# Sixth pair's projections, first output rows, and the three parts of a held group: three moves in the order of a layer-norm, state-space and mixture-of-experts kernel

## The chip, the cores and the metric

One core of a Trainium2 chip runs the whole program. The metric is the device time of one execution in microseconds (us). A span is the time from the first to the last instruction of one profiled execution; the device time of that execution is a little longer.

## The reference, cut to what matters

For 16 sequences of 512 tokens with 256 numbers each:

```python
xn = layernorm(x)
# state space: Bu = xn @ B_w.T (64 states), h[t] = sigmoid(log_lambda) * h[t-1] + Bu[t]
y  = h @ C_w.T + D * xn
# mixture of experts, 8 experts, top 1, with a capacity for each expert and sequence
aff      = (xn @ waff.T) / (|xn| * |waff| + 1e-9)
tcr      = one_hot(argmax(softmax(aff)))
cap      = clip(floor(512 * sigmoid(mean(aff) - threshold)), 4, 512)
dispatch = tcr * (rank of aff along the sequence < cap)
ffn = sum over e of ( gelu((xn * dispatch[e]) @ W1[e] + b1[e]) @ W2[e] + b2[e] )
out = x + y + ffn
```

An expert maps 256 to 1024 to 256. A token that an expert does not take still gets that expert's answer to a zero row, so the kernel gives every token the sum of all experts' answers to zero (`call`) and, for a token that was taken, adds its own expert's answer less that expert's answer to zero (`zb`).

## The kernel before, in words

**Front.** The 16 sequences are eight pairs of sequences, numbered q = 0 to 7 (HQ = 4, so HQ + 2 is pair 6 and HQ + 3 is pair 7). For each pair, `load_x` fetches the rows and `load_xt` the transposed rows, 1 MB each, over SP's DMA queue. `project` (L243) multiplies the transposed rows by `proj`: part 0 gives the affinity numerators in a bank of `ps_m`, part 1 the 64 state inputs in a bank of `ps_f`, both banks single; ScalarE (ACT) copies each out (`npart`, `bur`), and ACT's queue writes `npart` to `numr`. `scaled` brings the norms to the other layout, `recur` (L359) multiplies and scans on VectorE (DVE), and `outputs` (L367) multiplies a pair's states by C_w in two parts (`py`, 8 matmuls each), copies them on ACT and writes the rows to `row_d`. `py0` shares its bank with the norms of pair 1 until `recur(1)` has read them.

**Routing and steps.** `first_routing` gives the first half of the tokens to 9 groups of two tiles of 128 tokens ("pairs", steps 0 to 8). `second_routing` packs the rest into 23 pairs (steps 9 to 31) and single tiles (steps 32 to 36). A step does, for its group: `turned` transposes the normalised rows (`px` on TensorE (PE), copied to `xsT` on DVE) one step ahead; `hidden` (L882) runs four stages 0 to 3 of W1 (`ph`, then Gelu on ACT into `hs`), and then one stage for each tile (4, and 5 for a pair) of W2 (`po`). After each stage a function `between(stage, event)` issues what is to lie there: weights for step i + 2 (`fetched`, four parts, SP queue), row gathers for step i + 3 (`gathered`, GpSimd (POOL), one indirect DMA for a tile), the transposes for step i + 1, and in steps 0 to 3 what the front has left over (`left_out`, L1329: outputs and recurrences of the pairs). Steps 0 to 8 keep their answers (`held_y`); the rows of `row_d` and the capacities are not ready yet.

**Dealt work.** From step 1 on three generators, `capacity` (L1002), `second_routing` (L637) and `capacity_mask` (L1048), are dealt out by `fill` (L1213) after each stage. A ledger `lead` sets how much: `pe(...)` adds what PE work has been issued, `dve(...)` takes off what DVE work has been issued, and `fill` draws from the first generator that is not waiting while `lead` is above 0. A generator that yields a number has issued that much DVE work; one that yields `None` is passed over for the rest of this call. What of `lead` is not drawn is dropped. Before step 9 `drained` (L1228) issues all that is left, with no stage between.

**Held groups.** From step 10 on the held groups j = 0 to 8 are finished beside the later steps, in three turns: turn 0 gathers their two tiles of x rows, turn 1 their two tiles of `row_d` rows (both on POOL, behind the last stage's event), turn 2 loads the expert's `zb1`, and at the step's end does the DVE work `normal`, `rests`, `finish` and the two scatters to the output. `held_turns` (L1411) says which turns lie beside which step: even groups have turns 0 and 1 beside one step and turn 2 beside the next, odd groups one beside each of three, all of it beside the pairs, steps 10 to 31.

Within the two blocks the order on PE, DVE, POOL and SP is the order of the text, each engine and each queue taking its own in order. A PSUM bank of a pool with one buffer is given on when the last reader of its tile is done: `pn`, `pp`, `pv2`, `ps_s` and `pk` use that of `ps_m`; `pa`, `pm` and the accumulator `pz` of the bias shares (from step 4 on) use that of `ps_f`.

Of the kernel before, what the change touches and what calls it, by code (L numbers as in the profile page):

```python
# [15 lines left out]
P = 128  # L16
B, S, D = 16, 512, 256
NS = 64
# [41 lines left out]
def ssm_moe_kernel(  # L60
# [166 lines left out]


    NQ = B // 2
    known, nparts = {}, {}  # L230
    xts, x4s, burs, hTs, halfs, prss, rows_out = {}, {}, {}, {}, {}, {}, {}

    def load_x(q, x4=None):
        for h in range(2):
            t = x4[h] if x4 else fx.tile([P, NC, D], F32, name="x4", bufs=4)
            nc.sync.dma_start(out=t, in_=xp[q].rearrange("p (h c d) -> p h c d", h=2, c=NC)[:, h])
            x4s[q, h] = t

    def load_xt(q, xt2=None):
        xts[q] = xt2 or fx.tile([P, 2, ND, S], F32, name="xt2", bufs=2)  # L240
        nc.sync.dma_start(out=xts[q], in_=xt[q].rearrange("p (h dc s) -> p h dc s", h=2, dc=ND))

    def project(q, parts=(0, 1)):  # L243

        for part in parts:
            pb = (ps_m, ps_f)[part].tile([P, S], F32, name="pb", tag="mf"[part])
            pe(1.9)
            m = (32, NS)[part]
            cols = slice(0, NS) if part else slice(NS, NS + m)
            for dc in range(ND):  # L250
                for h in range(2):
                    nc.tensor.matmul(
                        out=pb[h * m : (h + 1) * m, :],
                        lhsT=proj[:, dc, cols],
                        rhs=xts[q][:, h, dc, :],
                        start=(dc == 0),
                        stop=(dc == ND - 1),
                    )
            if part:
                burs[q] = held.tile([P, S], F32, name="bur", tag="y")  # L260
                nc.scalar.copy(burs[q], pb)
                continue
            npart = nparts[q] = fin.tile([2 * m, S], F32, name="npart", bufs=2)
            nc.scalar.copy(npart, pb[: 2 * m, :])
            if q >= NQ // 2:
                for h in range(2):
                    k = 2 * q + h
                    nc.scalar.dma_start(out=numr[k * NE : (k + 1) * NE, :], in_=npart[h * m : h * m + NE, :])
# [149 lines left out]
    def ranks(hf, rt, banks, tags):  # L418
# [33 lines left out]
        if hf:  # L452
            pn = banks[0].tile([P, NC, HB * NE], F32, name="pn", tag=tags[0])
            rows = slice(hf * HB * NE, (hf + 1) * HB * NE)
            numc = numr.rearrange("k (c p) -> k c p", c=NC)
            for c in range(NC):
                nc.tensor.transpose(pn[:, c, :], numc[rows, c, :], ident[rows, rows])
            yield None
        aff3 = aff[:, hf].rearrange("p c b e -> p (c b) e")
        if hf:  # L460
            nc.vector.tensor_tensor(aff3, den, pn.rearrange("p c (b e) -> p (c b) e", e=NE), ALU.mult)
# [369 lines left out]
        return load_w2, products, folded, shares  # L831


    def behind(transfer, event):

        if event is not None:
            tc.add_manual_dep(
                transfer.ins,
                event.ins.name,
                mybir.DependencyInfo(mybir.DependencyClass.Sync, mybir.DependencyReason.DATA),  # L840
                reason="begun where the queues have room",
            )

    def gather(t, src, idx, event=None):
        begun = nc.gpsimd.indirect_dma_start(  # L845
            out=t, out_offset=None, in_=src, in_offset=bass.IndirectOffsetOnAxis(ap=idx, axis=0)
# [155 lines left out]
    def capacity(mk):  # L1002

        while "affinities" not in known:
            yield None
        affc = mk.tile([P, NC, P], F32, name="affc", tag="affc")
        nc.vector.tensor_copy(
            affc.rearrange("p c (h k) -> p h c k", h=2), aff.rearrange("p h c b e -> p h c (b e)")
        )
        yield 0.8  # L1010
        cap = small(mk, "cap", 1)
        col = small(mk, "col", 1)
        nc.vector.tensor_reduce(col, aff.rearrange("p h c b e -> p (h c b e)"), AX.X, ALU.add)
        yield 0.8
        yield None
        pa = ps_f.tile([P, S], F32, name="pa", tag="f")
        for c in range(NC):
            nc.tensor.transpose(pa[:, c * P : (c + 1) * P], affc[:, c, :], ident)
        row = known["row"] = mk.tile([P, S], F32, name="row")
        nc.vector.tensor_copy(row, pa)  # L1020
        yield 0.8
        yield None
        yield None

        pm = ps_f.tile([P, 1], F32, name="pm", tag="f")
        nc.tensor.matmul(out=pm, lhsT=ones, rhs=col, start=True, stop=True)
        yield None
        nc.vector.tensor_scalar(cap, pm, 1.0 / (NT * P * NE), thr_sb, ALU.mult, ALU.subtract)
        nc.scalar.activation(cap, cap, AF.Exp, scale=-1.0)
        yield 0.2  # L1030
        yield None
        yield None
# [12 lines left out]
        known["capacity"] = cap  # L1045
        yield 0.8
# [118 lines left out]
    def span(i):  # L1165

        g = order[i] - NP1
        return (2 * i, 2) if g < 0 else (2 * g, 2) if g < NP2 else (NP2 + g, 1)
# [65 lines left out]
    with front_pools:  # L1234
# [4 lines left out]
        with tc.manual_schedule(engines={PE, DVE, ACT, POOL, SP}):  # L1239
# [6 lines left out]
            def quarter(t, k):  # L1246
                return t[:, k * NC * D : (k + 1) * NC * D].rearrange("p (c d) -> p c d", c=NC)
# [11 lines left out]
            xt_late = [hid.tile([P, 2, ND, S], F32, name="xt_late", tag="hs") for j in range(2)]  # L1259
            load_x(HQ + 2, [quarter(x_late, k) for k in (0, 1)])  # L1260
            load_xt(HQ + 2, xt_late[0])
            load_x(HQ + 3, [quarter(x_late, k) for k in (2, 3)])
            load_xt(HQ + 3, xt_late[1])

            moments(0)
            roots(0)
# [22 lines left out]
            routing = first_routing(rt1)  # L1289
            for meanwhile in (  # L1290
                lambda: None,
                lambda: (project(HQ), recur(0), project(HQ + 1)),
                lambda: None,
            ):
                while next(routing) is not None:
                    pass
                meanwhile()
# [6 lines left out]
                    gathered(0, what, None, (s,))  # L1304
            scaled(2, ps_h, "ph")
            scaled(3, ps_h, "ph")
            project(HQ + 2)
            recur(1)
            recur(2)
            xns[0], events[0, "xn"] = normal(*rows[0][:2], 1)  # L1310
            first, events[0, "xsT"] = turned(xns[0], 1, ps_x)
# [1 line left out]
            recur(3)  # L1313
            gathered(1, 0, events[0, "xn"])
            gathered(1, 1, events[0, "xsT"])
            fetched(1, None, events[0, "xsT"])

            def second_tile():
                normal(*rows[0][:2], 2, 1, xns[0])
                turned(xns[0], 2, None, 1, first)  # L1320
                moments(HQ)
                roots(HQ)
                moments(HQ + 1)
                normed(1)
# [2 lines left out]


            left_out = {  # L1329
                (0, 0): [(0, 0)],  # L1330
                (0, 1): [(0, 1)],
                (0, 2): [(1, 0)],
                (0, 3): [(1, 1)],
                (0, 4): [(2, 0)],
                (0, 5): [(2, 1)],
                (1, 0): [(3, 0)],
                (1, 1): [(3, 1)],
                (2, 0): [(4, None)],
# [59 lines left out]
    with (  # L1398
# [8 lines left out]
        NW = 6  # L1407
        held_rows = {}


        held_turns = {}  # L1411
        beside = [i for i in range(NP1 + 1, steps) if span(i)[1] == 2]
        for j in range(NP1):
            for turns in ((0, 1), (2,)) if j % 2 == 0 else ((0,), (1,), (2,)):
                held_turns[beside.pop(0)] = j, turns
        with tc.manual_schedule(engines={PE, DVE, POOL, SP}):
            load_w2, products, folded, shares = bias_shares(fp)
            for k in range(3):
# [1 line left out]
            for i in range(EARLY, steps):  # L1420
# [11 lines left out]
                def between(stage, event):  # L1432
                    if stage < NPART:
                        fetched(i + 2, stage, event)
                    if stage == 1:
                        gathered(i + AHEAD, 0, event)
                        turn(i + 1, (ps_x, ps_x2)[i % 2])
                    if stage == 3:
                        gathered(i + AHEAD, 1, event)
                    for turn_of in turns:  # L1440
                        if turn_of == 2 or stage != (4 if turns == (0, 1) and turn_of == 0 else 5):
                            continue
                        if turn_of == 0:
                            held_rows[j] = rows_of(x_rows, row_d, inv1, 2 * j, 2, [event, event])
                        held_rows[j][2](turn_of)
                    k = stage - 2 + NW * (i - EARLY)
                    if 0 <= k < pieces:
                        products(k)
                        pe(0.6)
                        if k + 3 < pieces:  # L1450
                            load_w2(k + 3)
                    if k == pieces - 1:
                        folded()
                    if k == pieces + 2:
                        shares()
# [82 lines left out]
```

## Time and profile before

| | |
|---|---|
| median of 3 runs | 628.13 us (624.35 to 629.61) |
| the profiled execution's own time | 626.64 us |
| its span | 624.9 us |
| granted TensorE clock, mean | 0.988 |
| PE matmul busy | 591.9 us (95%) |
| DVE, ACT, POOL busy | 368.3, 169.5, 265.2 us |

Times in the views are counted from the span's start. A line of a timeline gives start, length, engine, line, operation, output and input tiles and how many instructions are merged; in brackets stands how long the engine was idle just before and what ended that. In a table by windows the figures are busy time of each engine, the granted clock of TensorE (1.00 is full), the share of the DMA engines' time and the rate in GB/s. Steps begin with PE's first `ph` of a group: step 0 at 60.70, step 3 at 126.42, step 9 at 247.76, step 10 at 263.77, step 11 at 278.02, step 31 at 567.82, and the singles 32 to 36 at 581.85, 589.10, 596.34, 603.59 and 610.83.

### The profile page before, as it was taken

The numbers are of one execution on the slowest core, as the hardware profiler recorded it, in microseconds if no ns is written. First come the engines' busy times: TensorE is split into PE (matmuls) and PEld (weight loads), VectorE is DVE, ScalarE is ACT, GpSimd is POOL, SyncE is SP. The second block draws the span as 40 slices with busy tenths as digits, with TensorE's granted clock in tenths as the row PEclk, the third lists the DMA queues.
The fourth block names the chain that finished last, engine by engine and source line by source line (L and its number), as shares of the span: only waits on it lengthen the run. The fifth ranks groups of instructions, "written<-read, shape, count | busy, mean of one in ns | idle before, by whom it ended". The sixth has DMA issues, their size and how long they took to land. (4 is left out here: it accounts for less than half of the span.)

```text
span 624.9 us, 9629 instructions
## 1 busy us (share of the span) xinstructions
PE 591.9 (95%) x3163; PEld 475.3 (76%) x3163; DVE 368.3 (59%) x975; ACT 169.5 (27%) x406; POOL 265.2 (42%) x274
## 2 busy tenths in 40 slices
PE   5877999989999998999999999999999999999995
PEld 2224768758776677888888888888888888888995
DVE  5976745499878876536347373546447374463541
ACT  2224533344112230222222222222222222222331
POOL 1104782212222121365565555665566655535511
PEclk9897999999999999999999999999999999999999
DMA  8986676857677642475676666766665766767790
GB/s 331 373 324 242 256 279 243 250 200 275 216 280 254 244 158 97 177 238 211 223 251 237 233 246 236 257 235 233 221 237 212 245 222 228 250 215 243 252 319 7
DMA packets 48260, 147.62 MB, mean 236 GB/s; under 512 B 8861, under 2 KB 14864, under 8 KB 46160
## 3 DMA queue, kind: packets, MB, share of 16 engines
q1 hardware_dynamic: 35072, 109.00, 48.5%
q0 software_dynamic: 11504, 29.10, 14.1%
q10 hardware_dynamic: 1632, 8.88, 3.7%
q8 instruction: 26, 0.43, 0.3%
q14 instruction: 26, 0.21, 0.1%
HBM read 129.81 MB, written 17.65 MB: 236 GB/s over the span
## 5 line engine op out<-in xcount | busy, mean ns | idle before, releaser
L898 PE MATMUL ph<-xsT,ws 128*128 128x256 f32 (+1 forms) x1216 | 259.8, 365 | 4.9 <-ACT hs L907 4.4
L918 PE MATMUL po<-ws,hs 128*128 128x256 f32 x1104 | 247.3, 380 | 0.0
L898 PEld LDWEIGHTS ph<-xsT,ws 128*128 128x128 f32 x1216 | 212.1, 191 | 39.4 <-ACT hs L907 7.4
L918 PEld LDWEIGHTS po<-ws,hs 128*128 128x128 f32 x1104 | 208.0, 190 | 32.0 <-issue 3.6
L907 ACT ACTIVATE hs<-ph,ws 128x256 f32<-128x256 f32 (+1 forms) x304 | 121.1, 451 | 327.5 <-issue 203.3
L845 POOL DMA_INDIRECT sums<-in_xp_dram,inv_g x51 | 53.9, 1058 | 77.3 <-ACT hs L907 62.9
L984 DVE TENSOR_TENSOR w<-po,zb 128x512 f32<-128x512 f32 (+1 forms) x28 | 18.0, 644 | 110.2 <-PE po L918 77.1
L845 POOL DMA_INDIRECT yr<-row_d,inv_g x51 | 51.2, 1005 | 53.5 <-ACT hs L907 40.4
L991 POOL DMA_INDIRECT out_dram<-sums,inv_s x51 | 51.1, 1002 | 51.4 <-DVE sums L987 38.3
L880 DVE COPY xsT<-px 128x512 f32<-128x512 f32 (+1 forms) x38 | 24.4, 641 | 78.5 <-PE px L876 44.9
L845 POOL DMA_INDIRECT xs<-in_xp_dram,inv x18 | 19.5, 1082 | 74.2 <-ACT hs L907 31.2
L987 DVE SCALAR_TENSOR_TENSOR sums<-w,mslot,sums 128x256 f32<-128x256 f32 x69 | 30.6, 482 | 1.3
L958 DVE TENSOR_SCALAR xn<-sums,yr 128x256 f32<-128x256 f32 x69 | 25.9, 414 | 6.8 <-DMA yr<-row_d,inv_g 6.8
L845 POOL DMA_INDIRECT st<-st_d,inv x18 | 18.0, 999 | 24.7 <-DVE cap_i L1037 9.5
L991 POOL DMA_INDIRECT out_dram<-sums,out x18 | 18.2, 1013 | 22.8 <-DVE sums L987 20.0
L845 POOL DMA_INDIRECT sums<-in_xp_dram,inv x18 | 17.0, 946 | 19.3 <-PE po L918 15.0
L975 DVE TENSOR_TENSOR sums<-sums,call 128x512 f32<-128x512 f32 (+1 forms) x37 | 24.3, 657 | 1.3
L974 DVE TENSOR_TENSOR sums<-sums,v 128x512 f32<-128x512 f32 (+1 forms) x37 | 24.3, 656 | 1.3
L972 DVE TENSOR_TENSOR sums<-sums,yr 128x512 f32<-128x512 f32 (+1 forms) x37 | 24.3, 656 | 1.2
L973 DVE TENSOR_TENSOR v<-xn,d_sb 128x512 f32<-128x512 f32 (+1 forms) x37 | 24.3, 655 | 0.0
L876 PE MATMUL px<-ident,xn 128*128 128x128 f32 x138 | 21.7, 274 | 2.5 <-DVE xn L958 2.4
L1079 DVE TENSOR_SCALAR_CACHE_REDUCE junk<-srow,cand 128x512 f32<-128x512 f32 x31 | 23.1, 746 | 1.1
(282 smaller groups left out, 409.7 us busy)
## 6 DMA issues: line engine op xcount, KB each, us to landing
ws<-in_w_dram SPq DMA_DIRECT2D x148, 513.0 KB
row_d<-yrow ACTq DMA_DIRECT2D x8, 1040.0 KB
x<-in_xp_dram SPq DMA_DIRECT2D x12, 512.0 KB
w2s<-in_w_dram SPq DMA_DIRECT2D x16, 384.0 KB
zb<-z_d SPq DMA_DIRECT2D x37, 128.0 KB
early<-in_xt_dram SPq DMA_DIRECT2D x4, 1024.0 KB
xt<-in_xt_dram SPq DMA_DIRECT2D x2, 1024.0 KB
x_late<-in_xp_dram SPq DMA_DIRECT2D x4, 512.0 KB
```

The costliest lines, as they stand in the source:

```text
L845: begun = nc.gpsimd.indirect_dma_start(out=t, out_offset=None, in_=src, in_offset=bass.IndirectOffsetOnAxis(ap=idx, axis=0))
L880: return into, nc.vector.tensor_copy(xsT[:, :, cols], px[:, :, cols])
L898: nc.tensor.matmul(out=ph[:, k, cols], lhsT=w1s[:, dc * NF + c * P : dc * NF + (c + 1) * P], rhs=xsT[:, dc, cols], start=(dc == 0), stop=( ...
L907: event = nc.scalar.activation(hs[:, c, cols], ph[:, k, cols], AF.Gelu, bias=b1s[:, c : c + 1])
L918: event = nc.tensor.matmul(out=po[:, s, :], lhsT=hs[:, c, s * P : (s + 1) * P], rhs=w2s[:, c * D : (c + 1) * D], start=(c == 0), stop=(c = ...
L958: event = nc.vector.tensor_scalar(xn[:, s, :], xs[:, s, :], st[:, s, 0:1], st[:, s, 2:3], ALU.subtract, ALU.mult)
L972: nc.vector.tensor_add(r, r, yr[:, :n, NST:])
L973: nc.vector.tensor_tensor(v[:, :n, :], xn[:, :n, :], over(d_sb), ALU.mult)
L974: nc.vector.tensor_add(r, r, v[:, :n, :])
L975: nc.vector.tensor_tensor(r, r, over(call), ALU.add)
L987: nc.vector.scalar_tensor_tensor(out=r[:, s, :], in0=v[:, s, :], scalar=mslot[:, k0 + s : k0 + s + 1], in1=r[:, s, :], op0=ALU.mult, op1=A ...
L991: put = nc.gpsimd.indirect_dma_start(out=out, out_offset=bass.IndirectOffsetOnAxis(ap=inv[:, k0 + s : k0 + s + 1], axis=0), in_=r[:, s, :] ...
```

## The change

- The projection matmuls of pair 6 (`project(HQ + 2)`) are issued straight behind those of pair 5, while the first routing is under way; their copies out of PSUM (`projected`) stay where they were. `outputs(0)` moves from stages 0 and 1 of step 0 to between `recur(1)` and `recur(2)`, ahead of step 0, and the other entries of `left_out` for step 0 move up by two stages.
- Pair 7's loads (2 MB) leave the first run of loads; they are issued in `second_tile`, behind the normalisation of step 0's second tile, and step 1's weights follow them on the same queue (before, these were issued behind the copy of the first tile).
- In the dealt work, `second_routing` waits three calls of `fill` rather than one between the transposes `pn` and the DVE work that reads them, and `capacity` four calls rather than none between `pa` and its reader.
- Each held group's three turns lie beside three steps in a row, from step 10 to step 36, single tiles among them.

```diff
-    def project(q, parts=(0, 1)):
+    def project(q, parts=(0, 1), copied=True):
         for part in parts:
-            pb = (ps_m, ps_f)[part].tile([P, S], F32, name="pb", tag="mf"[part])
+            pb = pbs[part] = (ps_m, ps_f)[part].tile([P, S], F32, name="pb", tag="mf"[part])
...
+            if copied:
+                projected(q, (part,))
+
+    def projected(q, parts=(0, 1)):
+        for part in parts:
+            pb = pbs[part]
...
                 nc.tensor.transpose(pn[:, c, :], numc[rows, c, :], ident[rows, rows])
-            yield None
+            for _ in range(3):
+                yield None
...
             nc.tensor.transpose(pa[:, c * P : (c + 1) * P], affc[:, c, :], ident)
+        for _ in range(4):
+            yield None
         row = known["row"] = mk.tile([P, S], F32, name="row")
...
             load_x(HQ + 2, [quarter(x_late, k) for k in (0, 1)])
             load_xt(HQ + 2, xt_late[0])
-            load_x(HQ + 3, [quarter(x_late, k) for k in (2, 3)])
-            load_xt(HQ + 3, xt_late[1])
...
-                lambda: (project(HQ), recur(0), project(HQ + 1)),
+                lambda: (project(HQ), recur(0), project(HQ + 1), project(HQ + 2, copied=False)),
...
             scaled(3, ps_h, "ph")
-            project(HQ + 2)
+            projected(HQ + 2)
             recur(1)
+            outputs(0)
             recur(2)
...
-            fetched(1, None, events[0, "xsT"])
             def second_tile():
-                normal(*rows[0][:2], 2, 1, xns[0])
+                _, event = normal(*rows[0][:2], 2, 1, xns[0])
+                load_x(HQ + 3, [quarter(x_late, k) for k in (2, 3)], event)
+                load_xt(HQ + 3, xt_late[1])
+                fetched(1, None, event)
...
             left_out = {
-                (0, 0): [(0, 0)],
-                (0, 1): [(0, 1)],
-                (0, 2): [(1, 0)],
-                (0, 3): [(1, 1)],
-                (0, 4): [(2, 0)],
-                (0, 5): [(2, 1)],
+                (0, 0): [(1, 0)],
+                (0, 1): [(1, 1)],
+                (0, 2): [(2, 0)],
+                (0, 3): [(2, 1)],
...
-        held_turns = {}
-        beside = [i for i in range(NP1 + 1, steps) if span(i)[1] == 2]
-        for j in range(NP1):
-            for turns in ((0, 1), (2,)) if j % 2 == 0 else ((0,), (1,), (2,)):
-                held_turns[beside.pop(0)] = j, turns
+        held_turns = {NP1 + 1 + k: (k // 3, (k % 3,)) for k in range(3 * NP1)}
...
-                        if turn_of == 2 or stage != (4 if turns == (0, 1) and turn_of == 0 else 5):
+                        if turn_of == 2 or stage != 3 + n:
                             continue
```

More of the change, by code (lines that the diff above doesn't have):

```diff
@@ L229, in ssm_moe_kernel, with behind, load_x @@
     NQ = B // 2
-    known, nparts = {}, {}
+    known, nparts, pbs = {}, {}, {}
     xts, x4s, burs, hTs, halfs, prss, rows_out = {}, {}, {}, {}, {}, {}, {}
-    def load_x(q, x4=None):
+    def behind(transfer, event):
+        if event is not None:
+            tc.add_manual_dep(
+                transfer.ins,
+                event.ins.name,
+                mybir.DependencyInfo(mybir.DependencyClass.Sync, mybir.DependencyReason.DATA),
+                reason="begun where the queues have room",
+            )
+    def load_x(q, x4=None, event=None):
         for h in range(2):
             t = x4[h] if x4 else fx.tile([P, NC, D], F32, name="x4", bufs=4)
-            nc.sync.dma_start(out=t, in_=xp[q].rearrange("p (h c d) -> p h c d", h=2, c=NC)[:, h])
+            behind(nc.sync.dma_start(out=t, in_=xp[q].rearrange("p (h c d) -> p h c d", h=2, c=NC)[:, h]), event)
             x4s[q, h] = t
@@ L258, in project @@
                     )
+            if copied:
[3 more added lines that the diff above has]
+            pb = pbs[part]
+            m = (32, NS)[part]
             if part:
@@ L831, in bias_shares @@
         return load_w2, products, folded, shares
[L834 to L842, printed above, removed]
     def gather(t, src, idx, event=None):
@@ L1408, in ssm_moe_kernel @@
         held_rows = {}
-        held_turns = {}
-        beside = [i for i in range(NP1 + 1, steps) if span(i)[1] == 2]
-        for j in range(NP1):
-            for turns in ((0, 1), (2,)) if j % 2 == 0 else ((0,), (1,), (2,)):
-                held_turns[beside.pop(0)] = j, turns
+        held_turns = {NP1 + 1 + k: (k // 3, (k % 3,)) for k in range(3 * NP1)}
+        assert NP1 + 3 * NP1 < steps
         with tc.manual_schedule(engines={PE, DVE, POOL, SP}):
```

## The prediction, made before the result was known

> **What bounds the kernel now.** I read the page's first part, then who waited for whom on PE, then PE's timeline for each wait, then the other engines there. The chain that ended last is no help here: it holds only the last scatter.
>
> ```profile
> span 624.9 us, 9629 instructions
> PE 591.9 (95%) x3163; PEld 475.3 (76%) x3163; DVE 368.3 (59%) x975; ACT 169.5 (27%) x406; POOL 265.2 (42%) x274
> ```
>
> PE is busy 95%, so a microsecond counts only if it leaves PE's order of work or closes one of PE's few waits.
>
> ```profile
> PE pv L625 <- DVE lo L545: 5.2, 3, 4.3
> PE ph L898 <- ACT hs L907: 4.4, 5, 1.0
> PE px L876 <- DVE xn L958: 2.4, 1, 2.4
> PE pk L1134 <- DVE mp L1142: 1.5, 5, 0.8
> ```
>
> Each line is a total, a number of waits and the longest. The change touches all four places. The first, in the front:
>
> ```profile
> 49.40 0.36 PE L625 MATMUL pv<-pt,lo 128*128 128x36 bf16 x8 [4.26 <-DVE lo L545]
> ...
> 51.92 3.68 PE L331 MATMUL prs<-ident,mvr 128*64 128x128 f32 x32
> 55.53 4.28 PE L252 MATMUL pb<-xt_late,proj 128*32 128x512 f32 x16
> 59.75 0.44 PE L876 MATMUL px<-ident,xn 128*128 128x128 f32 x2
> ```
>
> PE idles from 45.14 to 49.40; the projections of pair 6 (`xt_late`) come later, right before `px`. The same 32 `prs` matmuls took 2.07 at 20.63, so 3.68 is a slow clock:
>
> ```profile
> 46.00:48.00 2.00, 0.00 (x0) 0.00 (x0) 1.97 (x4) 1.95 (x7) 0.00 (x0) 1.00 0.98 303
> 50.00:52.00 2.00, 1.28 (x26) 1.02 (x28) 1.07 (x2) 1.54 (x4) 0.00 (x0) 0.50 0.78 293
> 54.00:56.00 2.00, 2.00 (x18) 1.39 (x16) 1.97 (x3) 0.00 (x0) 1.64 (x2) 0.50 1.01 408
> ```
>
> Third figure from the end: the granted clock, 1.00 in the hole and 0.50 from 50 to about 57. The other places, from PE's and DVE's timelines:
>
> ```profile
> 58.83 0.41 DVE L958 TENSOR_SCALAR xn<-xs,st 128x256 f32<-128x256 f32 x1 [2.72 <-DMA st<-st_d,inv]
> ...
> 122.01 0.69 DVE L1020 COPY row<-pa 128x512 f32<-128x512 f32 x1 [8.31 <-PE pa L1018]
> ```
> ```profile
> 132.49 0.87 PE L876 MATMUL px<-ident,xn 128*128 128x128 f32 x4 [2.35 <-DVE xn L958]
> ```
> ```profile
> 243.81 0.89 PE L1134 MATMUL pk<-mp,lo 128*128 128x53 bf16 x16 [0.77 <-DVE mp L1142]
> ...
> 284.75 1.99 PE L898 MATMUL ph<-xsT,ws 128*128 128x256 f32 x8 [0.83 <-ACT hs L907]
> ```
> ```profile
> 595.28 0.41 DVE L958 TENSOR_SCALAR xn<-sums,yr 128x256 f32<-128x256 f32 x1 [3.55 <-DMA yr<-row_d,inv_g]
> ```
>
> In order: the first tile's `xn` waits for a gather; DVE stands 8.3 us in its own order for `pa`, and `xn` of step 4 behind it makes PE wait 2.35; the drain before step 9 goes at DVE's pace; a hole of 0.83 to 0.84 stands in steps 11, 16, 21 and 26, each right after a step with turns 0 and 1 together; and among the singles gathered rows come late.
>
> **The change part by part.** The sum is made against the profiled execution, 626.64 us (span 624.9); that is 1.5 below the median of 628.13, within the runs' 624.35 to 629.61.
>
> *A. Front.* Pair 6's 16 projection matmuls take 3.75 (half of 7.49 for 32 at 37.65), so from 45.14 they end at 48.9, inside the hole; they wait for ACT's copies of pair 5, done at 43.9 and 45.9, and for `xt_late`, whose load was issued at 32.85, before the DMA share sank to 0.20 at 42 to 44. `pv` is set by DVE's `lo` and stays. PE's path from 51.92 is then `prs` (2.07 to 3.68), half of `outputs(0)` 1.13, two ACT copies 1.07, the other half 1.13: 5.4 to 7.0, so PE is free for `px` at 57.4 to 59.0. `xn` needs the gather of `st`, issued by 55.05, landed at 58.8 while the DMA share was 1.01; pair 7's 2 MB, now not ahead of step 0's weights, free that stretch. Landing lies between 55.05 and 58.8, so `px` starts between 57.4 (the PE path) and 59.3 against 59.75: a gain of 0.45 to 2.3. I take 1.5, between the ends, since the clock can go either way. ACT's Gelu table load (1.28) follows the last `py` copy as it now follows `bur`: no cost. `outputs(0)`'s 2 x 1.13 leave step 0: 2.27 more. Of the rest, pair 7's three loads and step 1's four weight loads queue on SP from about 61: 4.2 MB at the 300 to 400 GB/s shown is 11 to 14 us, landing by 75; first needed are the moments of pair 7 (78.3 now, the rows come first) and step 1 (88.46 now), so nothing. POOL's gathers for step 1 keep their order and start earlier. Together -3.8 (-2.7 to -4.6).
>
> *B. Later reading of `pn` and `pa`.* DVE no longer stands for `pa`. Walking the ledger call by call (it reproduces where `pn`, `pp`, `pa`, `pm`, `ps_s` and `pk` now stand), `pa` falls to step 2 stage 5 and its reader to step 3 stage 4. Behind `pp` DVE then has `recur(6)` 1.9, 2.3 of `run` to `left` and `xn` 0.73, some 5 us, where PE has 9 before `px` of step 4. So -2.35 (0 to -2.35: next late would be `xn` again).
>
> *C. `pm` meets `pz`.* By the ledger `pm` falls to step 4 stage 1, its reader on DVE to stage 2; there the products of the bias shares first use the same bank and must wait for that reader. DVE has `xsT` 0.69, 1.7 of `eq` and `pt`, and `cap` 0.21 behind `px`; PE 0.27 and 1.95. Cost 0.45 (0 to 1.5, if DVE lags). Behind the waiting products PE's whole order is held.
>
> *D. Drain.* The three calls for `pn` drop some 6 us of the ledger (nothing else can be dealt there), so the mask comes later: by the ledger `ps_s` falls to step 8 stage 5, and `own`, `mtok` and the four `mp` of the first table join the drain. Now the second table's `mp` start 0.48 after step 8's last `po` (242.69) and step 9's `ph` at 247.76. Then: `ps_s` 0.64 to `own`, 0.72 and 0.72 for `own` and `mtok`, then the four `mp` of 0.27, each pair waiting for a `pk` of 0.35, and `mslot` 0.18, about 2.0: the second table's start moves 3.6 later. PE's 0.44 for `ps_s` and 0.95 of `pk` leave step 8. Net +2.2 (1.3 to 3.9: step 9's first 16 `ph` take 5.37 at half clock there, 3.62 later, so 1.75 of slow clock may come on top or half of it go).
>
> *E. Holes.* Four of 0.84 follow steps with eight gathers in one go on POOL (four of the step, four held); the 12 steps of odd groups, six gathers or fewer, show none. The change has six at most, so all go: -3.35 (0 to -3.35; not below, as nothing else stands there).
>
> *F. Held groups among the singles.* Turn 2 is DVE's 0.73 + 2.75 + 1.57 = 5.05. A single step has 7.25 of PE and 3.4 of DVE. Group 7's `row_d` rows are gathered at 589.7 to 592.0, behind step 35's; those were issued 588.0 to 589.0 and read at 595.28, 6.3 later, so group 7's come at 598.3 and its DVE work ends at 603.4. `finish` of step 33 and `xsT` of step 35 queue behind it: 0.9 + 0.42 gives 604.75 where PE wants it at 603.59: 1.2 (0 to 2.5). On POOL four scatters, group 8's x rows and a scatter then push its `row_d` gathers to 611.0 to 613.5. DMA is idle by then (share 0.10); landed at 615.2, 5.05 of DVE, then the last step's 0.9, to 621.15; three scatters, last at 622.5 against 619.42. So +3.1 at the end with the 1.2 in it (2.0 to 4.0). The earlier pair steps carry no more than odd groups now do: nothing.
>
> Sum: -3.8 - 2.35 + 0.45 + 2.2 - 3.35 + 3.1 = -3.75, so 622.9.
>
> A rule at the clock: the rows show 0.50 from 50 to 57 after a hole of 4.26, and 0.50 from 248 to 251 behind the drain. [...]
>
> **The rivals.**
>
> *Holes stay (chance 0.2).* They could come from the state of PE's signals, not from the gathers: ACT and DVE, waiting for PE, both go on at 283.9, though PE's row ends its first stages earlier. Against it: exactly the four steps behind double turns. 622.9 + 3.35 = 626.2.
>
> *Slower: late rows among the singles (0.12).* DMA share is 0.93 to 1.00 from 590 to 608, and groups 7 and 8 add eight gathers of 0.13 MB. Each microsecond that group 7's rows land after 597 passes through DVE's order to `xsT` of step 35 and so to PE. From a landing 10.1 after issue (6.3 + 3.8) the kernel is slower than before; at double the latency, 12.6, it is 622.9 + 6.3 = 629.2. Against it: the extra bytes are some 12% of the 2.2 MB that a single step moves.
>
> *The clock stays halved (0.12).* [...] A at -2.7, D at +3.9: 622.9 + 1.1 + 1.7 = 625.7.
>
> *The front and the tail at their good ends (0.15).* Gather at once, `xsT` of step 35 in time: A -4.6, F +2.0, D +1.3: 622.9 - 0.8 - 1.1 - 0.9 = 620.1.
>
> **How the numbers follow.** My forecast has 0.41: 622.9, by itself 621 to 625. Leaving out about 0.1 at each side, 619.5 to 629.0 takes in the good end and all but the far part of the late rows. About 1% (6.3) of the median is what a measurement can tell from no change: faster means below 621.85, slower above 634.4. Below 621.85 lie most of the good end and a third of the forecast, 0.28; above 634.4 only an extreme of the late rows, 0.03; 0.69 between.
>
> **What would show it.** A: no hole of 4 us before `pv`, clock 1.00 at 50 to 53, step 0 starting at 58.5 to 60, step 1 some 4 us earlier. B: no wait at `px` in step 4. C: a wait of about 0.5 at the first `pz`. D: `ps_s` behind step 8's last `po`, some 8 us of sparse `pk`. E: no holes of 0.84 every fifth step. F: a wait for `xsT` at step 35, three scatters after the last `po`. I am wrong if the holes come back elsewhere, if the bank of `pm` costs PE more than 2 us, or if step 35 waits more than 4.

## The result, and the profile after

The changed kernel takes 623.96 us (median of 20 runs, 617.9 to 630.02) beside 626.48 for the kernel before on the same chips (20 runs). The ratio is 0.9939, with a 95% interval of 0.9918 to 0.996: about 0.6% faster, inside the 1% called no change. The ratio is taken over fast executions alone, which leaves out four of the changed kernel (627.2 to 630.02). The profiled execution has a span of 620.9, 4.1 below that of before, where the sum had forecast 3.75 less. That the sum came out so close is in part luck: by the table below A and E came out 1.8 and 1.4 better than forecast, and F 3.0 worse.

PE's step starts (first `ph` of a group) cut both spans into the same stretches:

| stretch | before | after | difference | forecast |
|---|---|---|---|---|
| start to step 1 | 88.46 | 82.83 | -5.63 | A -3.8 |
| step 1 to step 8 | 136.62 | 134.40 | -2.22 | B, C -1.9 |
| steps 8 and 9, with the drain | 38.69 | 41.10 | +2.41 | D +2.2 |
| step 10 to step 31 | 304.05 | 299.31 | -4.74 | E -3.35 |
| step 31 to the last `po` | 50.34 | 56.46 | +6.12 | F +3.1, tail included |
| last `po` to the end | 6.77 | 6.77 | 0.00 | in F |

The first part of the page shows that most of this is PE's waiting; its work is the same 3163 matmuls, and it is busy only 0.8 less:

```profile
span 620.9 us, 9634 instructions
PE 591.1 (95%) x3163; PEld 475.9 (77%) x3163; DVE 369.7 (60%) x975; ACT 169.9 (27%) x406; POOL 262.8 (42%) x274
```

A. PE's timeline of the changed front. The hole of 4.26 ahead of `pv` has become 0.56, and `py` (the first output rows) stands ahead of `px`:

```profile
48.01 0.37 PE L644 MATMUL pv<-pt,lo 128*128 128x36 bf16 x8 [0.56 <-DVE lo L564]
...
50.49 3.00 PE L349 MATMUL prs<-ident,mvr 128*64 128x128 f32 x32
53.42 1.72 PE L399 MATMUL py<-cw_sb,hT 64*128 64x256 f32 x8
55.82 1.61 PE L399 MATMUL py<-cw_sb,hT 64*128 64x256 f32 x8 [0.67 <-ACT yrow L403]
57.36 0.44 PE L885 MATMUL px<-ident,xn 128*128 128x128 f32 x2
58.32 2.05 PE L907 MATMUL ph<-xsT,ws 128*128 128x128 f32 x16 [0.52 <-issue]
```

The same place by windows; the third figure from the end of a row is the granted clock:

```profile
50.00:52.00 2.00, 1.92 (x34) 1.79 (x32) 1.33 (x4) 0.66 (x2) 0.73 (x1) 0.81 0.11 34
52.00:54.00 2.00, 2.00 (x17) 1.60 (x16) 1.97 (x3) 0.70 (x2) 1.39 (x3) 0.50 0.30 83
54.00:56.00 2.00, 1.33 (x9) 0.82 (x6) 1.09 (x2) 0.82 (x2) 1.69 (x2) 0.84 0.04 1
```

A mean of 0.81 over 2 us is 0.76 us of half clock; with 2.0 and 0.64 from the other rows that is 3.4 us, where before had about 7.

B and C. PE's timeline at step 4's transposes, with no wait in brackets any more, and at the first product of the bias shares, with a new one:

```profile
124.35 0.60 PE L885 MATMUL px<-ident,xn 128*128 128x128 f32 x4
...
146.87 0.61 PE L829 MATMUL pz<-w2s,gb 128*8 128x256 f32 x6 [0.67 <-ACT hs L916]
```

The row names ACT's `hs`, but that one runs until 147.08; the reader of `pm` on DVE, whose bank `pz` takes over, ends at 146.77, 0.10 ahead of `pz`.

D. The drain on PE: `ps_s` and the first table's `pk` have joined it, behind the last `po` of step 8:

```profile
230.78 2.75 PE L927 MATMUL po<-ws,hs 128*128 128x256 f32 x12
233.37 0.60 PE L1125 MATMUL ps_s<-ident,sel 128*128 128x128 f32 x4
235.81 0.56 PE L1145 MATMUL pk<-mp,lo 128*128 128x18 bf16 x16 [1.84 <-DVE mp L1153]
236.57 0.56 PE L1145 MATMUL pk<-mp,lo 128*128 128x18 bf16 x16 [0.20 <-DVE mp L1153]
237.90 0.89 PE L1145 MATMUL pk<-mp,lo 128*128 128x53 bf16 x16 [0.77 <-DVE mp L1153]
...
242.25 5.45 PE L907 MATMUL ph<-xsT,ws 128*128 128x256 f32 x16
```

E and F. From step 10 to step 31 PE waits nowhere. Among the singles it waits four times:

```profile
579.68 1.13 PE L927 MATMUL po<-ws,hs 128*128 128x256 f32 x4 [1.46 <-ACT hs L916]
...
587.04 1.99 PE L927 MATMUL po<-ws,hs 128*128 128x256 f32 x8 [0.48 <-issue]
...
600.92 1.16 PE L907 MATMUL ph<-xsT,ws 128*128 128x128 f32 x8 [1.71 <-issue]
...
604.94 1.99 PE L927 MATMUL po<-ws,hs 128*128 128x256 f32 x8 [1.13 <-ACT hs L916]
```

Steps 32, 33 and 35, in which they stand, take 8.98, 8.23 and 10.65 in place of 7.25, which makes the 6.1. None of the four is the forecast wait for `xsT`. ACT's timeline says what ACT waited for:

```profile
579.26 0.63 ACT L916 ACTIVATE hs<-ph,ws 128x128 f32<-128x128 f32 x2 [2.97 <-PE po L927]
...
600.24 0.63 ACT L916 ACTIVATE hs<-ph,ws 128x128 f32<-128x128 f32 x2 [2.24 <-PE ph L907]
```

In step 32 PE's last two `ph` that ACT waits for had ended at 575.40 and 575.62; the Gelu starts at 579.26, 3.6 later, though ACT has nothing else to do. The trace also records when PE's signal (the semaphore that ACT, DVE and POOL wait on) was raised. Six raises stand due, and none is made until all six are, together:

```
signalling matmuls of PE end: 575.40 575.62 576.92 577.35 577.78 578.22
PE's signal is raised:        579.19 579.24 579.31 579.36 579.40 579.44
```

POOL's row shows a run of five indirect transfers, with no more than 0.3 between them, from 572.11 that ends at 578.23, 0.96 before the first raise. The trace does not hold every raise (331 for 382 signalling matmuls), so a signal is called late below only where an engine that waits for it starts late too.

### The profile page after: what moved, and what is told of

It is laid out like the page before. It is cut to its first block, busy times and chain, and to the rows that moved or that the text cites. A ratio compares the mean times of both kernels' runs of the same rounds, so it can differ in the third digit from the quotient of the medians.

```text
span 620.9 us, 9634 instructions
## 1 busy us (share of the span) xinstructions
PE 591.1 (95%) x3163; PEld 475.9 (77%) x3163; DVE 369.7 (60%) x975; ACT 169.9 (27%) x406; POOL 262.8 (42%) x274
## 5 line engine op out<-in xcount | busy, mean ns | idle before, releaser
L854 POOL DMA_INDIRECT sums<-in_xp_dram,inv_g x51 | 51.7, 1014 | 72.0 <-ACT hs L916 50.5
L403 ACT COPY yrow<-py 128x512 f32<-128x512 f32 x32 | 17.2, 591 | 17.8 <-PE py L399 14.5
```

The lines of the kernel that those rows point to most:

```text
L854: begun = nc.gpsimd.indirect_dma_start(out=t, out_offset=None, in_=src, in_offset=bass.IndirectOffsetOnAxis(ap=idx, axis=0))
```

## The experiments

**The parts.** The first four kernels put the change together from its parts.

e1: the changed kernel with the held turns of before.

```diff
-        held_turns = {NP1 + 1 + k: (k // 3, (k % 3,)) for k in range(3 * NP1)}
-        assert NP1 + 3 * NP1 < steps
+        held_turns = {}
+        beside = [i for i in range(NP1 + 1, steps) if span(i)[1] == 2]
+        for j in range(NP1):
+            for turns in ((0, 1), (2,)) if j % 2 == 0 else ((0,), (1,), (2,)):
+                held_turns[beside.pop(0)] = j, turns
...
-                        if turn_of == 2 or stage != 3 + n:
+                        if turn_of == 2 or stage != (4 if turns == (0, 1) and turn_of == 0 else 5):
```

> The changed kernel with the held turns of the kernel before (two parts together beside every even group, all beside pairs): the parts A to D alone. Theory (long runs of POOL's indirect transfers make PE's signals late, and a long run stands behind a double turn and, in the changed kernel, among the singles): steps 10 to 30 get the four holes back, +4.7 against the changed kernel, and the singles take 50.3 again in place of 56.5, -6.1: about 1.4 below the changed kernel, 622.5, singles 50.3. Rival (the singles' 6.1 come from what the front and drain shifted, not from the held work): the singles stay near 56 and the time is 4.7 above the changed kernel, 628.7.

e2: the kernel before with the held turns of the changed one (the same edit, the other way).

> The kernel before with only the held turns of the changed kernel: parts E and F alone. Theory: -4.7 in steps 10 to 30, +6.1 among the singles: about 1.4 above the kernel before, 627.9. Rival (the gain in steps 10 to 30 or the loss among the singles depends on the rest of the change): between 621.7 (only the gain) and 632.6 (only the loss).

e4: one waiting call for `pn`, four for `pa`.

```diff
-            for _ in range(3):
-                yield None
+            yield None
```

> The changed kernel with one waiting call between the transposes pn and their reader again (before: one, changed: three), the four calls for pa kept. Theory (the three calls drop part of the ledger, which pushes the mask's first table into the drain): the drain before step 9 is 2.3 shorter, the wait at px of step 4 stays away since it was pa's: 2.3 below the changed kernel, 621.7. Rival (the later reading of pn is what removed the wait of 2.35 at px in step 4): the drain's 2.3 are won and 2.35 lost again, no difference.

e5: the kernel before with the front of the changed one.

> The kernel before with part A alone (projections of pair 6, first output rows, pair 7's loads); pn, pa and the held turns as before. Theory (A is worth about 3.9 up to the start of step 1, read from profiles of four kernels with A and two without; the four holes and the wait at px of step 4 stay): 3.9 below the kernel before, 623.5. Rival (part of A's gain is given back in steps 1 to 9, by pair 7's late loads or since the drain takes up what the front leaves): 1 to 2 below, 626; or the wait of 2.35 at px in step 4 goes with A alone, 621.1.

The kernels ran on several chips, each beside the kernel before (medians there 626.61 to 628.91), so the ratios are what compares. The last four columns are from the profiles.

| kernel | median us | ratio to before (95%) | step 1 starts | steps 1 to 9 | 10 to 30 | 31 to last `po` |
|---|---|---|---|---|---|---|
| before | | | 88.46 | 175.31 | 304.05 | 50.34 |
| changed | 623.96 | 0.9939 (0.9918 to 0.996) | 82.83 | 175.50 | 299.31 | 56.46 |
| e1 | 623.19 | 0.9939 (0.9913 to 0.9964) | 85.98 | 175.18 | 304.06 | 50.34 |
| e2 | 627.75 | 1.0015 (0.999 to 1.0039) | 88.72 | 175.88 | 299.30 | 54.00 |
| e4 | 621.42 | 0.9912 (0.988 to 0.9944) | 85.78 | 171.98 | 299.31 | 56.29 |
| e5 | 623.35 | 0.9946 (0.9922 to 0.997) | 84.90 | 175.45 | 304.02 | 50.34 |

The front alone (e5) is worth 626.61 x 0.0054 = 3.4, and the wait at `px` of step 4 stays in it, 2.35. Its ratio lies inside the changed kernel's interval: the other three parts together bring nothing that can be told from noise. The held turns bring the four holes back in e1 and take them away in e2, 4.75 each time; they cost 6.1 among the singles in the changed kernel and 3.7 in e2. So they are no gain: in e1, without them, the kernel is as fast as the changed one within the interval (1.4 less had been expected, which these times could not tell). In e4 the wait at `px` stays away though `pn` is read as early as before, so it was the calls for `pa` that removed it, and those for `pn` are what lengthens steps 1 to 9, by 3.5. The rival expected of e4 (won and lost again) is refuted by the profile; the intervals of the two ratios overlap, so the times alone would not show it.

**What makes the holes.** e3, e6 to e8, e10 and e11 ask what the held parts do to PE.

e3: held work beside pairs only, no step with two gathering turns, turn 2 of an even group beside turn 0 of the next.

```diff
...
+        for j in range(NP1):
+            for turn_of in range(3):
+                held_turns.setdefault(at, []).append((j, turn_of))
+                if turn_of < 2 or j % 2 == 1:
+                    at += 1
...
```

> The changed kernel with all held work beside pairs again, steps 9 to 31, never two gathering turns beside one step: turn 2 of an even group lies beside the same step as turn 0 of the next group, so that in such a step POOL issues six gathers and four scatters rather than eight gathers and two scatters. Theory 1 (what makes PE's signals late is a long unbroken run on POOL, and the scatters of turn 2 come at another time of the step, after DVE's work): no holes among the pairs but perhaps half of them, singles back at 50.3: about 6 below the changed kernel, 618. Theory 2 (the count of indirect transfers in a step decides, ten as before): four holes of 1.2 come back: -6.1 + 4.9, about 622.8. Rival (DVE's held work makes the late signals): as theory 2 or more, since DVE's work then falls together with gathers.

Measured 621.55, ratio 0.9908 (0.9879 to 0.9937). The singles are back at 50.34, and two steps behind each of the four merged ones stands a step of 14.89 to 14.95, 0.67 too long: half a hole, between the two theories, so this one told them apart poorly.

e6: e1, with the held gathers of the double turns as plain transfers on SP's queue.

```diff
...
+                            t, src = ((held_rows[j][0], x_rows), (held_rows[j][1], row_d))[turn_of]
+                            begun = nc.sync.dma_start(out=t[:, s, :], in_=src[(2 * j + s) * P : (2 * j + s + 1) * P, :])
...
```

> The kernel of the first experiment (held turns as before, five double turns), with the eight row transfers of each double turn's two gathering parts issued as plain transfers on SP's queue rather than as indirect ones on POOL: the same bytes at the same event, POOL's run shorter by four. The held tokens of the even groups take other rows than theirs. Theory 1 (POOL's indirect transfers make PE's signals late): all four holes of 1.2 go, steps 11, 16, 21 and 26 at 14.25, 617.7 to 618.5 against 623.2. Theory 2 (the load on the DMA engines does it): the holes stay, 15.4.

e7 and e10: e1, with three or five fills on POOL for each such gather.

```diff
...
+                            for k in range(3):
+                                behind(nc.gpsimd.memset(t[:, s, :], 0.5), event if s == k == 0 else None)
```

> The kernel of the first experiment, with the four indirect transfers of each double turn replaced by twelve fills of the same tiles on POOL (about 0.4 each from the fill of a 128 x 128 tile at 0.20, so 4.7 of unbroken work, as the transfers were 5.0): POOL's run as long as before, four transfers fewer. The held tokens of the even groups are computed from constants. Theory 1a (POOL's run as such makes PE's signals late): holes of about 1.2 stay behind steps 10, 15, 20 and 25. Theory 1b (the indirect transfers do it, by their number in a row): the holes go, steps at 14.25.

> As the experiment with fills on POOL, but twenty fills for each double turn, 6.8 at the 0.34 that one took there, so that POOL has no pause between its own gathers, the fills and the scatters behind them, as it had none in the kernel with indirect transfers (the earlier fills left one of 1.4). The held tokens of the even groups are computed from constants. Theory 1a (any unbroken run of POOL): the four holes of 1.2 come back. Theory 1b (indirect transfers alone, by their number in a row): no holes, 14.25 for steps 11, 16, 21 and 26.

e8: the changed kernel, with the gathers of groups 7 and 8 beside the singles on SP's queue, by the edit of e6.

> The changed kernel with the held gathers beside steps 31, 32, 34 and 35 (groups 7 and 8) issued as plain transfers of other rows on SP's queue; DVE's held work and its scatters stay. Theory 1 (POOL's indirect transfers in long runs): the singles go from 56.5 back to 50.3 or, since the four held scatters stay, to 52: 4.5 to 6 below the changed kernel, 618 to 619.5. Theory 2 (the bytes): the singles stay near 56, 624. Rival 3 (DVE's held work of step 33, which lies in the way of what the singles need): the waits of step 35 stay, some 3.4, and those of steps 32 and 33 go: 621.

e11: e1, with the first part of a double turn behind stage 2.

```diff
-                        if turn_of == 2 or stage != (4 if turns == (0, 1) and turn_of == 0 else 5):
+                        if turn_of == 2 or stage != (2 if turns == (0, 1) and turn_of == 0 else 5):
```

> The kernel of the first experiment with the first part of a double turn behind stage 2 in place of stage 4: the same ten indirect transfers beside the step, but the four held gathers no longer stand in a row behind the step's own four. Theory (how many stand in a row decides): the holes shrink or go, steps 11, 16, 21 and 26 between 14.25 and 14.9, 618 to 621. Rival (the number beside a step decides, in any order): holes of 1.2 as in the first experiment, 623.

| kernel | median us | ratio to before (95%) | steps 10 to 30 | 31 to last `po` |
|---|---|---|---|---|
| e6 | 618.65 | 0.9854 (0.9813 to 0.9894) | 299.30 | 50.35 |
| e7 | 617.49 | 0.9858 (0.9818 to 0.9897) | 299.30 | 50.34 |
| e8 | 620.0 | 0.9873 (0.984 to 0.9906) | 299.30 | 51.42 |
| e10 | 618.76 | 0.9832 (0.9804 to 0.9859) | 300.04 | 50.34 |
| e11 | 619.11 | 0.9838 (0.981 to 0.9865) | 299.41 | 50.34 |

The same bytes on another queue make no holes (e6, e8), and fills on POOL at the same place, 7.0 us without a pause in e10, make none behind a double turn (e7, e10). Nor do the fills hold up a signal: in e10's first double turn they run from 273.20 to 280.22, three signalling matmuls end meanwhile (276.58, 278.31 and 280.04), and each signal is raised within 0.02. So the holes take POOL's indirect transfers. (The medians of e6, e7 and e10 hold another 1.8 that is not the holes': behind the last `po` they take 4.9 to 5.0, e1 6.8. Why was not asked.) How they reach PE can be read in e1. POOL's timeline, eight transfers with no more than 0.4 between them, beside steps 10 and 11:

```profile
269.81 0.94 POOL L854 DMA_INDIRECT yr<-row_d,inv_g  x1 [1.64 <-ACT hs L916]
...
276.14 0.95 POOL L854 DMA_INDIRECT yr<-row_d,inv  x1 [0.30 <-issue]
277.39 1.01 POOL L1000 DMA_INDIRECT out_dram<-sums,inv_s  x1 [0.30 <-issue]
278.71 1.01 POOL L1000 DMA_INDIRECT out_dram<-sums,inv_s  x1 [0.30 <-issue]
```

PE, then ACT, then DVE of e1 at the same time:

```profile
278.86 0.60 PE L885 MATMUL px<-ident,xn 128*128 128x128 f32 x4
279.30 1.96 PE L907 MATMUL ph<-xsT,ws 128*128 128x256 f32 x8
282.11 1.99 PE L907 MATMUL ph<-xsT,ws 128*128 128x256 f32 x8 [0.84 <-ACT hs L916]
```

```profile
281.22 1.57 ACT L916 ACTIVATE hs<-ph,ws 128x256 f32<-128x256 f32 x4 [2.00 <-remote]
```

```profile
281.27 0.69 DVE L889 COPY xsT<-px 128x512 f32<-128x512 f32 x1 [4.06 <-PE ph L907]
```

PE's transposes `px` are over at 279.46. DVE's copy of them starts at 281.27 and ACT's next Gelu at 281.22, at the same moment and 1.5 behind the end of POOL's run (279.72), though neither engine had anything else to do. PE runs on, needs a bank that ACT should have emptied, and stands.

e11 has a run of eight as well, from 266.72 to 276.55, and there too the signals are held: PE's `po` of step 10 ends at 276.37, and DVE's `w`, which reads it, starts at 278.29, 1.7 behind the run:

```profile
278.29 0.69 DVE L993 TENSOR_TENSOR w<-po,zb 128x512 f32<-128x512 f32 x1 [8.10 <-PE ph L907]
```

But the only other signal that fell due is that of a `ph` that ends at 278.10; nobody waits for that `w` soon, and ACT's Gelu starts at 278.44, so that PE goes on. So the holes went, as e11's theory had it, but not for its reason: eight still stand in a row. The place of the run's end in the step decides what it costs, not whether signals are late. The kernel before holds the same comparison: its four runs of eight end 4.31 into steps 11, 16, 21 and 26, which have the holes; three runs of ten end 13.39 into steps 13, 23 and 28, and PE goes on into the next step. The first of the three ends with this line of POOL's, and PE begins the next step at 322.00 with no wait in brackets:

```profile
320.19 0.94 POOL L845 DMA_INDIRECT yr<-row_d,inv  x1 [0.30 <-issue]
```

```profile
322.00 3.62 PE L898 MATMUL ph<-xsT,ws 128*128 128x256 f32 x16
```

Over the fourteen profiles 18 of the pair steps from 10 to 30 take 14.36 or more, all others 14.25, and the 18 are exactly those in which a run of six transfers or more ends 1.05 to 4.32 behind the step's start. e10 gives the counter-proof by accident. At one place its fills hold back POOL's later work, so that beside steps 26 and 27 two scatters, four gathers and four scatters join to a run of ten. It ends in step 27's W1 stages, the signals come 1.3 later, at 509.80, and the one hole of e10 stands there, in a step where e1 has none:

```profile
507.50 0.99 POOL L1000 DMA_INDIRECT out_dram<-sums,inv_s  x1 [0.30 <-issue]
510.93 0.98 POOL L854 DMA_INDIRECT sums<-in_xp_dram,inv_g  x1 [2.44 <-ACT hs L916]
```

```profile
510.71 1.56 PE L907 MATMUL ph<-xsT,ws 128*128 128x256 f32 x6 [0.47 <-ACT hs L916]
```

e3's merged steps fit too: a run of twelve from 288.71 that ends at 304.18, in the W1 stages, signals at 305.90. What inside the chip ties PE's signals to POOL's transfers stays open, and so does the shortest run that does it: a run of six that ends 4.33 into step 31 of the kernel before makes PE wait nowhere, while runs of five cost time among the singles.

**Two repairs.** e9: held turns one beside each step from step 6 on, a third part beside step 9, none beside singles; `pn` as in e4.

```diff
...
+        for i, part in ((6, (0, 0)), (7, (0, 1)), (8, (1, 0)), (9, (0, 2)), (9, (1, 1)), (10, (1, 2))):
+            held_turns.setdefault(i, []).append(part)
+        for j in range(2, NP1):
+            for turn_of in range(3):
+                held_turns[at] = [(j, turn_of)]
+                at += 1
...
```

> The changed kernel with the held turns one beside each step from step 6 to step 31 (beside step 9, which has no scatters of its own, a third and a gathering turn of two groups), none beside the singles, and pn read after one waiting call as before. In no step does POOL issue more than eight indirect transfers. Theory (more than eight in a run make the holes; a third, DVE's part at step 9, is hidden): no holes among the pairs, singles as in the kernel before (36.3 from step 32 to the last po in place of 42.4), the shorter drain of the pn experiment: 6.1 and 2.5 below the changed kernel, 615. Rival (the held gathers beside steps 6 to 9 delay the gathers that steps 9 to 12 need, or DVE's 5 us beside step 9 make step 10 wait): 2 to 5 of it lost again, 617 to 620.

e12: e11 with `pn` as in e4.

> The two cheapest repairs together: the changed front and the four calls for pa kept, pn read after one waiting call as before, the held turns all beside pairs as before, with the two parts of a double turn behind stages 2 and 5 rather than 4 and 5. Theory (the repairs add up: no holes as in the experiment with the parts apart, a drain shorter by 3.4 as in the pn experiment): 619.1 less 3.4, 615.7, by the same ratio to the kernel before 0.979. Rival (the absence of holes with the parts apart hung on where the steps stood, and they come back when all is moved by 3.4): up to 4.8 more, 620.5.

e9 takes 616.77, ratio 0.9802 (0.978 to 0.9825); e12 616.08, ratio 0.9814 (0.9782 to 0.9845). Both beat the kernel before and the changed one, whose interval (0.9918 to 0.996) lies clear of theirs. e9 loses 2.5 against e4 in steps 1 to 9 (174.51 for 171.98), as its rival had it. Neither has a hole from step 10 on; e12 has steps 1 to 9 in 171.99, as e4. PE's waits in e12 from step 8 to the last `po`, all that are left:

```profile
PE pk L1144 <- DVE mp L1152: 1.3, 4, 0.8
```

## Why the prediction came out as it did, point by point

**A, right in size, its clock wrong.** Part of the profile's -5.63 up to step 1 is not the change's: the first `pv` starts at 48.01 there, at 49.40 in the kernel before, and anywhere from 47.37 (e12) to 50.57 (e10) in the others with the same front. From the first `pv` to step 1 the twelve kernels with this front take 34.8 to 36.6, the kernel before 39.06: a gain of 2.5 to 4.3. e5's 3.4 in time stands against the forecast 3.8. The division was off: from the first `pv` to `px` it is 9.35 in place of 10.35, so 1.0 and not 1.5 came ahead of `px`, and step 0 lost 3.25, where 2.27 had been worked out; the rest is the wait of 1.02 for ACT in step 0 that is absent in the profile (and present in e5, 1.25). One cost is in no term of A: in eight of the twelve, e5 among them, PE stands 1.9 to 2.0 between the halves of `py` in place of 0.67, as ACT's copy starts late (in e5 at 56.13, behind a `py` that ended at 54.85). POOL issues eight gathers in a row there; that this is the lateness of E and F again is likely, and not shown. The hole is gone, but the clock is not full: one stretch of 3.4 us at half clock (51.25 to 54.66) stays in this profile, with no wait of 1 us ahead of it, only thin `pv`. That is chance as much as the change: e5 and e8, with the same front, have no such stretch there, and e1, e6, e10 and e11 have one of 6.8 (57.0 to 63.8 in e1). The clock of 1.00 at 50 to 53 that I had forecast from the closed hole fits e5 and e8, where the 32 `prs` take 1.97, and not this profile, where they take 3.00 and the rows show 0.81, 0.50 and 0.84. That a closed hole alone gives the full clock was my estimate, and these rows do not bear it out.

**B, right.** `px` of step 4 does not wait, and e4 and e5 show that it is the reading of `pa` alone.

**C, right.** 0.67 for 0.45, behind the reader that was named. In e4, where `pn` is read early, `pz` does not wait.

**D, right.** 2.41 for 2.2. The windows from 238 to 246 show 0.74, 0.50, 0.50 and 0.55, two stretches of half clock where there was one (6.83 us, from 238.98, beside 3.4), as the worse end of D's range had it, but step 9's first 16 `ph` take 5.45 as against 5.37, so the further one fell on `pk` that wait for DVE anyway.

**E, right place, price three tenths too low, cause half right.** I priced a hole by the idle time before one `ph`, 0.84. But the four steps behind a double turn took 15.43 to 15.47 where the others take 14.25, 4.77 together, of which 4.74 shows; what the idle time leaves out is in small delays that no row names as waiting. And "eight gathers in one go" was not the cause as such: e11 has them without a hole, e3 and e10 have holes with other transfers, and three of the steps with six gathers or fewer, which I took for harmless, hold runs of ten.

**F, the step that failed.** The forecast had PE waiting 1.2 for `xsT` at step 35 and 1.9 at the tail, 3.1 in all, with the holes of E gone for good; a price for late signals of PE was not in it. Measured are 6.1, and no tail. DVE's and POOL's times came as forecast: counted from step 31, group 7's rows were to land 30.5 behind it (598.3 less 567.82) and DVE read them at 30.8 (588.41 less 557.64); group 8's `row_d` gathers were to run from 43.2 to 45.7 and ran from 43.3 to 45.5. But PE itself was late by then. On POOL the held gathers and scatters and the singles' own transfers, which come every 7.25 in place of 14.25, joined to runs of five and more, and the held-up signals cost 6.1: a run of five, 6.1 long, is nearly as long as a single step, so that its end can hardly miss the stages in which PE needs ACT (this is my reading; no run varies the place among the singles). PE's lateness covered the wait and the tail that I had priced: the forecast wait is in none of PE's rows, and behind the last `po` nothing was added. e8, which takes the held gathers off POOL, uncovers the forecast wait, at step 35, where DVE's held work of group 7 stands ahead of the copy:

```profile
596.90 2.05 PE L907 MATMUL ph<-xsT,ws 128*128 128x128 f32 x16 [0.76 <-DVE xsT L889]
```

```profile
594.78 0.88 DVE L996 SCALAR_TENSOR_TENSOR sums<-w,mslot,sums 128x256 f32<-128x256 f32 x2
...
596.43 0.42 DVE L889 COPY xsT<-px 128x256 f32<-128x256 f32 x1
```

The singles of e8 take 51.42, 1.08 more than before: beside the 1.2 that I had worked out. Behind the last `po` e8 takes 7.1, 0.35 more than before; but there group 8's rows do not queue on POOL, which is what the tail of 1.9 was made of, so its price stays untested.

The rival that the holes stay, "from the state of PE's signals, not from the gathers", had half of it: they are PE's signals, and they did come back elsewhere, but the transfers make them. Holes that come back elsewhere were the prediction's own first sign of being wrong. By setting the two against each other I came to look for holes only where eight gathers meet, and not among the singles.

## What to carry to other kernels

When an engine stands for another that had finished by its own row, look at who else waits for that engine: in e1 ACT and DVE woke at 281.22 and 281.27, 1.5 behind the end of POOL's run, and the reason was there and not in the engine that the row names. Price such a hole by the length of the whole step beside a clean one (15.43 to 15.47 beside 14.25, where the idle time shows 0.84). And before work is moved to where steps are short (7.25 in place of 14.25 here), lay out in time what the same queue issues there already: one part to a step still made one unbroken run (five transfers, 6.1 long), and what a run cost hung on where in the step it ended (among the pairs a hole at 1.05 to 4.32 behind the start, none at 13.39).

## What the runs showed of the hardware that I had not expected

- PE's signals were held up while POOL issued an unbroken run of indirect transfers, and were raised 1.0 to 1.9 us after its end, in these places: 0.96 in the changed kernel's step 32 (a run of five), 1.1 behind a run of six in e9, 1.5 behind eight in e1, 1.7 in e11, 1.9 in e12 (a run that ends at 340.80, a raise at 342.67). One was raised late inside a run as well (the changed kernel's 600.22, 2.2 behind its `ph`). In e9 it cost nothing: in step 12 the last Gelu of W1 starts at 295.73, 1.5 behind its `ph`, while PE is busy with W2.

```profile
292.50 0.84 ACT L915 ACTIVATE hs<-ph,ws 128x256 f32<-128x256 f32 x2 [1.33 <-PE ph L906]
295.73 0.84 ACT L915 ACTIVATE hs<-ph,ws 128x256 f32<-128x256 f32 x2 [2.40 <-remote]
```

- The order alone is worth 4.65 us in the profiles (304.06 to 299.41 for steps 10 to 30): e11 differs from e1 by one digit, and 0.9939 of the kernel before became 0.9838; the intervals do not overlap.
- Half clock came in stretches of 3.4 us or a double one: 25.9 to 29.3, 49.8 to 56.6 and 247.7 to 251.2 in the kernel before, 23.94 to 27.35, 51.25 to 54.66 and 238.98 to 245.81 in the changed one, and 57.0 to 63.8 in e1's front; a last one, from 623.2 and from 617.9, lasts to the end of the span. In both kernels' profiles the changes of the granted clock lie whole multiples of 3.41 us apart. No wait over 0.77 us stands in the 3.4 us ahead of 51.25; in e8, with the same three waits at `pv` (0.56, 0.77 and 0.23), the 32 `prs` take 1.97 and not 3.00, so that the waits alone do not tell which profile has the stretch. What does is not shown.
